# Graph attention over 16 images: setup bursts in pairs over two sets of PSUM banks, and loads and copies moved between queues

## The chip, the cores and the metric

The kernel runs on one core of a Trainium2 chip. A core has engines that run side by side, each in its own order: TensorE (PE, matmuls, with PEld for its weight loads), VectorE (DVE), ScalarE (ACT), GpSimd (POOL) and SyncE (SP), which here only issues DMA transfers. On-chip memory is SBUF; matmuls write to PSUM, which has eight banks of 512 floats in each of 128 partitions. The metric is the device time of one execution in microseconds (us).

## The reference

The input is 16 images of 512 rows and 512 features, one vector q of 512 for each image, and for each image an integer label array of 512 x 512 x 11. What is computed, cut to what matters:

```python
row_zero = v.sum(-1) == 0
q_exp = jnp.where(row_zero[..., None], 0.0, q[:, None, :])
self_feat = jnp.concatenate([v, q_exp], -1) @ W_self.T + b_self
output = self_feat
for d in range(2):                      # adj, and adj transposed
    A = (adj if d == 0 else jnp.swapaxes(adj, 1, 2))[:, :, :20, :]
    output += gat(self_feat, A.sum(-1), A @ w_bias + b_bias, Wq[d], ..., Wout[d], bout[d])
return v + relu(output)

def gat(x, cond, label_bias, ...):      # 16 heads of 32
    kv = x[:, :20]                      # the first 20 rows are the keys
    aff = einsum("bnhd,bmhd->bnhm", q, k) / sqrt(32)
    w = softmax(where(cond > 0, aff, NEG) + label_bias)
    return einsum("bnhf,hgf->bnhg", einsum("bnhm,bmf->bnhf", w, kv), Wout) + bout
```

So every image has 512 queries against 20 keys, 16 heads and two directions: 640 scores a row. The condition row_zero asks for each row of v whether its sum is zero; the kernel keeps that as "flags", one number for each row, by which q's part is multiplied.

## The kernel before

All arithmetic is float32 (F = 512 features are held as C = 4 chunks of 128 partitions). Nothing is scheduled by a planner: `manual_schedule` leaves each engine's instructions in the order in which they are written, and each DMA is issued by the engine whose queue it is written to. A helper `behind` gives a load on SP's queue another instruction to wait for, so that loads start in turn. An instruction that waits holds up all that follows on its engine or queue.

**The setup** (lines 458 to 777) loads the weights, computes the self features of the 16 x 20 key rows (`kv_terms`, L537), the 8 blocks of projected keys khD (`key_rows`, L588), and then, in 20 bursts, the keys multiplied back through Wq (`keys`, L676), so that the loop can take scores directly from self features. A burst is 25 or 26 units, a unit being 19 columns (keys 1 to 19 less key 0) of one image, direction, head group and feature chunk; its four heads are row-tiled matmuls with a contraction of 32 that run side by side in the array, 475 or 494 columns long. They write into two tiles of two PSUM banks each from the pool ps_s. ACT then scales and copies the pair of heads 0 and 1 (L691), DVE the pair of heads 2 and 3 (L693), into a stage tile st in SBUF. A stage is 32 units; when it is full, POOL copies image 0's part to g0 (L697) and SP stores image 1's part to g1_d (L698) and the other 14 images to g_d (L699), 1064 KB, in DRAM. There are 16 stages.

Between bursts PE does other work, here called filler, which is column-tiled (32 columns of output for each of four tiles) and writes to a pool of four more banks: the remaining key rows, `values` (L649: the keys' values through Wout, stored to vw_d), `bias_scores` (L624), and the block products of image 0 (L283). A string `plan` lists the filler behind each burst. Two of the fillers, `row_flags` of images 0 and 1 (L213), use the whole array: a 128 x 128 matrix of ones times the row sums (which POOL has added up in `row_sums`), so that each partition of a 512-column bank holds the sums of all rows; DVE's comparison with zero writes the flags nz[b], [128, 512], straight into SBUF (L215).

The values must reach bd_d in DRAM in block-diagonal form: `clear_first` writes zeros there (POOL's queue), and 12 DRAM-to-DRAM copies (`spill`, L187; the list `copies` from `blocks(0)`) put the values of the first five images in their places. Six of them are issued on POOL's queue in the setup (after bursts 14 to 19) and six in the loop.

**The loop** (lines 786 to 1006) goes over images b (16) and row tiles nt (4 of 128 rows). A row tile has 64 score matmuls into two banks (`scores`, L365, some 4 us) and a softmax: DVE adds the mask and bias (L379), takes the maximum (L383), subtracts it (L387), ACT exponentiates (L392), DVE sums and inverts (L415, L416), POOL multiplies (L417), DVE transposes (L424). In between PE makes the self features of image b + 1 by seven block products of Strassen's kind (`product`, L283, some 1.66 us each), which share four banks: products 1, 6, 7 and 4 add up in the pair ps_a, product 2 goes to ps_d, 5 and 3 to ps_c. After products 1, 6, 7 and 4 DVE reads the pair and adds flags times q (`partial`, L289) to give a block of the self features. The order is

```python
# nt == 2: scores(b, 2); product(b+1, 1); product(b+1, 2); weigh(b, 2) with partial(b+1, 0, 0) inside
# nt == 3: product(b+1, 6); normal(b, 2); partial(b+1, 0, 1); scores(b, 3); product(b+1, 7); product(b+1, 5); ...
```

and `attend` (L435, weights times values) of image b - 1 comes ahead of the scores of row tile 2. SP's queue carries, in the written order, the loads of labels (`load_adj`, L119), of bias scores (`load_cq`, L124), of x in two layouts (L107, L113), of keys g (`load_keys`, L135), values (L141) and flags (`load_nz`, L202), the zeros for the rest of bd_d (L157), copies (L187), and the stores of the result (L454). For images 2 and on the flags come from ACT's row sums: `row_mask` writes 512 of them to nz_d (L198) and `load_nz` reads them back to all partitions an image later.

## Time and profile before

| what | value |
|---|---|
| median of 3 runs | 583.28 us (582.72 to 583.82) |
| profiled execution | 582.57 us, span 580.7 us, granted clock 0.999 |
| busy share of PE, DVE, ACT, POOL | 99%, 84%, 68%, 70% |
| setup (to the first score matmul of the loop) | 91.3 us |
| bytes moved | 123.26 MB, 212 GB/s on average |

The span is that of the profiled instructions; the time of the execution includes what lies around it. A row of the timeline or of the chain begins with its start and its length in us, then the engine, the line and what is written from what. "SPq" and the like are an engine's queue of DMA issues: its length there is the time for which the issue occupied the queue, not the transfer's. In rows of groups, "busy, mean ns | idle before, releaser" tells the time and what the engine waited for; in those of one tile or line, three numbers are the least, median and greatest length in ns, followed by the starts of the first and the last. ps_k, ps_v, ps_nz, ps_a, ps_c, ps_d are the banks of key rows, values, flags and products; matmuls of float32 appear as two instructions each.

### The profile page before, as it was taken

The numbers are of one execution on the slowest core, as the hardware profiler recorded it, in microseconds if no ns is written. First come the engines' busy times: TensorE is split into PE (matmuls) and PEld (weight loads), VectorE is DVE, ScalarE is ACT, GpSimd is POOL, SyncE is SP. The second block draws the span as 40 slices with busy tenths as digits, with TensorE's granted clock in tenths as the row PEclk, the third lists the DMA queues.
The fourth block names the chain that finished last, engine by engine and source line by source line (L and its number), as shares of the span: only waits on it lengthen the run. The fifth ranks groups of instructions, "written<-read, shape, count | busy, mean of one in ns | idle before, by whom it ended". The sixth has DMA issues, their size and how long they took to land.

```text
span 580.7 us, 30994 instructions
## 1 busy us (share of the span) xinstructions
PE 574.0 (99%) x13496; PEld 431.6 (74%) x13496; DVE 489.8 (84%) x786; ACT 395.8 (68%) x1170; POOL 404.2 (70%) x383
## 2 busy tenths in 40 slices
PE   8999999999999999999999999999999999999996
PEld 6444458878878787878778787887887878787873
DVE  0475676979898989898999999898989898989896
ACT  1334454587877777778786868687887877777671
POOL 2626976748687776858585867786868677685875
PEclk9999999999999999999999999999999999999999
DMA  8998997857675767777576767566657666674404
GB/s 290 387 399 300 332 362 274 231 144 222 202 239 177 215 200 198 218 181 229 171 215 166 219 166 219 166 205 181 202 162 223 197 191 182 196 205 109 148 19 146
DMA packets 98787, 123.26 MB, mean 212 GB/s; under 512 B 18876, under 2 KB 66968, under 8 KB 96604
## 3 DMA queue, kind: packets, MB, share of 16 engines
q1 hardware_dynamic: 96124, 117.80, 65.5%
q0 software_dynamic: 1392, 2.43, 1.8%
q8 instruction: 106, 1.74, 1.2%
q10 hardware_dynamic: 1136, 1.06, 0.5%
q14 instruction: 29, 0.24, 0.1%
HBM read 82.30 MB, written 40.24 MB: 211 GB/s over the span
## 4 chain that ended last, share of the span: by engine, by line
PE 94%; DVE 3%; DMA 1%; issue 0%; POOL 0%; SPq 0%; ACT 0%; DVEq 0%; POOLq 0%; ACTq 0%
PE ps_s L365 45%; PE ps_a L283 19%; PE ps_c L283 9%; PE ps_o L435 5%; PE ps_d L283 5%; PE ps_v L649 3%; PE ps_k L588 3%; DMA ws_q<-in_wsT 1%; PE ps_kv L537 1%; DVE o L444 0%; PE ps_nz L213 0%; DVE o L1023 0%; DVE wt L424 0%; DVE ps_s L383 0%; DVE sm L415 0%
## 5 line engine op out<-in xcount | busy, mean ns | idle before, releaser
L365 PEld LDWEIGHTS ps_s<-g,sf 128*32 128x32 f32 x8192 | 263.0, 110 | 21.5 <-issue 13.9
L365 PE MATMUL ps_s<-g,sf 128*32 128x152 f32 x8192 | 278.1, 293 | 0.3 <-issue 0.2
L337 ACT COPY both<-add 32x80 f32<-32x80 f32 x512 | 130.9, 256 | 60.3 <-DVE add L328 54.4
L417 POOL TENSOR_TENSOR s<-s,sm 128x640 f32<-128x640 f32 x63 | 80.2, 1274 | 95.5 <-DVE sm L416 73.4
L344 POOL TENSOR_TENSOR full<-cq,both 128x640 f32<-128x640 f32 x64 | 100.3, 1567 | 27.1 <-issue 21.2
L317 ACT ACTIVATE prod<-adj,wb_sb 128x80 f32<-128x80 int32 x330 | 112.4, 432 | 0.0
L392 ACT ACTIVATE s<-s 128x640 f32<-128x640 f32 x63 | 46.5, 738 | 56.5 <-DVE s L387 56.1
L449 POOL TENSOR_TENSOR o<-o,x 128x512 f32<-128x512 f32 x60 | 76.6, 1299 | 0.0
L379 DVE TENSOR_TENSOR full<-ps_s,full 128x608 f32<-128x608 f32 x63 | 48.7, 773 | 22.5 <-PE ps_s L365 19.2
L283 PE MATMUL ps_a<-t,ws_s 128*32 128x246 f32 x1024 | 60.0, 371 | 0.0
L415 DVE TENSOR_REDUCE sm<-s 128x32 f32<-128x640 f32 x63 | 50.8, 807 | 10.6 <-ACT s L392 10.4
L383 DVE TENSOR_REDUCE ps_s<-full 128x32 f32<-128x640 f32 x63 | 52.2, 828 | 2.2
L424 DVE STREAM_TRANSPOSE wt<-s 128x640 f32<-128x640 f32 x63 | 52.8, 838 | 0.6 <-POOL s L417 0.6
L387 DVE TENSOR_TENSOR s<-full,ps_s 128x640 f32<-128x640 f32 x63 | 51.5, 818 | 1.1
L289 DVE SCALAR_TENSOR_TENSOR sf<-nz,qw,ps_a 128x246 f32<-128x246 f32 x128 | 51.6, 443 | 0.3
L283 PEld LDWEIGHTS ps_a<-t,ws_s 128*32 128x32 f32 x1024 | 33.9, 110 | 17.5 <-issue 0.9
L328 DVE TENSOR_REDUCE add<-prod 128x80 f32<-128x960 f32 x32 | 36.8, 1149 | 6.8 <-ACT prod L317 4.0
L446 ACT ACTIVATE o<-o,bo 128x512 f32<-128x512 f32 x60 | 38.2, 709 | 0.6 <-DVE o L444 0.6
L248 POOL TENSOR_TENSOR t<-x 128x492 f32<-128x492 f32 x32 | 36.7, 1148 | 1.6 <-DMA g_d<-st 1.5
L248 POOL TENSOR_TENSOR t<-x,t 128x492 f32<-128x492 f32 x32 | 36.7, 1148 | 1.3
L435 PE MATMUL ps_o<-wt,vd 32*32 32x512 f32 (+5 forms) x816 | 37.6, 578 | 0.0
L444 DVE TENSOR_TENSOR o<-ps_o,sf 128x512 f32<-128x512 f32 x60 | 36.7, 668 | 0.0
(225 smaller groups left out, 712.6 us busy)
## 6 DMA issues: line engine op xcount, KB each, us to landing
g<-g_d SPq DMA_DIRECT2D x60, 304.0 KB
g_d<-st SPq DMA_DIRECT2D x16, 1064.0 KB
out_T<-o SPq DMA_DIRECT2D x60, 256.0 KB
xn<-in_xn SPq DMA_DIRECT2D x56, 256.0 KB
x<-in_xT SPq DMA_DIRECT2D x56, 256.0 KB
adj<-in_adj SPq DMA_DIRECT2D x60, 220.0 KB
nz<-nz_d SPq DMA_DIRECT2D x14, 256.0 KB
wk<-in_wkT SPq DMA_DIRECT2D x2, 1024.0 KB
```

What stands on the lines that cost most here:

```text
L248: done["xsum"] = nc.gpsimd.tensor_sub(t, one, two)
L283: nc.tensor.matmul(to, lhs, x[:, k], start=start, stop=stop, skip_group_check=n != 2)
L289: done["partial"] = nc.vector.scalar_tensor_tensor(to[:, i], nzs[b][:, half(l)], qw[:, 2 * f + i, b : b + 1], parts[b, "a"][i][:, :HN], AL ...
L317: nc.scalar.activation(p[:, :, l], a[:, :, l], AF.Identity, scale=wb_sb[:, l : l + 1])
L337: done["spread"] = nc.scalar.copy(adds[b, h][bass.ts(a, R), :, g], add[r].rearrange("p (t m) -> p t m", t=2))
L344: done["full"] = nc.gpsimd.tensor_add(f, cqs[b].unsqueeze(1).to_broadcast(shape), adds[b, nt // 2][:, nt % 2].unsqueeze(2).to_broadcast(sh ...
L365: nc.tensor.matmul(to, sfs[b][:, k, bass.ds(nt * P + (2 * g + j) * R, R)], of, start=(onto is None and k == 0 and (whole or j == 0)), stop ...
L383: nc.vector.tensor_reduce(mx, f, AX.X, ALU.max)
L417: done["normal"] = nc.gpsimd.tensor_mul(s, s, sm.unsqueeze(3).to_broadcast(full))
L424: nc.vector.transpose(wts[b][:, nt], s.rearrange("p a h m -> p (a h m)"))
L435: nc.tensor.matmul(banks[a][bass.ds(at // 2 * DH, n * DH)].rearrange("p (t n) -> p t n", n=32), vd[r, bass.ds(at * DH, n * DH)], wt[r, :, ...
L449: nc.gpsimd.tensor_add(o[:, c], o[:, c], xs[b][:, c])
```

## The change

- The pool ps_s is opened after the setup. In the setup all eight banks form two pools of four single-bank tiles, `acc[0]` and `acc[1]`; a burst takes one set, a head to a bank.
- The bursts come as seven doubles and six singles: the string at the end of the diff lists them with their filler, "+" for a double. A double's second burst takes the other set, and the filler takes the set that was emptied first.
- Evictions go head by head in the order 0, 2, 1, 3 (ACT 0 and 1, DVE 2 and 3): 8 to 12 instructions a burst in place of 4 to 6.
- `row_flags` uses four column-tiled matmuls of 128 columns, compares a [128, 128] tile, writes 512 flags to nz_d, and `load_nz` reads them back. Image 0's are made in the setup; image 1's in the loop, at b = 0: written ahead of scores(0, 2), read back behind them.
- The loads of adj(0, 1) and x(1) and `clear_first` move to behind burst 14 (`later`). The 12 copies of `blocks(0)` are all issued on SP's queue, in row tile 0 of image 0, between the halves of load_adj(1, 0).
- `row_sums(1)` moves to the end of the setup; the pool xsum is opened ahead of work; `attend` does the runs of two first.

```diff
@@ -60,13 +60,13 @@
     load = ctx.enter_context(tc.tile_pool(name="load", bufs=2))
     sfp = ctx.enter_context(tc.tile_pool(name="sfp", bufs=3))
     msk = ctx.enter_context(tc.tile_pool(name="msk", bufs=2))
-    ps_s = ctx.enter_context(tc.tile_pool(name="ps_s", bufs=2, space=PSUM))
     acc = {}
 
     def bank(name, at=None):
 
-        tag = {} if at is None else {"bufs": 1}
-        return acc["pool"].tile([P, 512], F32, tag="acc" if at is None else f"acc{at}", name=name, **tag)
+        if at is None:
+            return acc[acc["from"]].tile([P, 512], F32, tag="acc", name=name)
+        return acc["pool"].tile([P, 512], F32, tag=f"acc{at}", name=name, bufs=1)
 
     ctx.enter_context(tc.manual_schedule())
 
@@ -208,11 +208,14 @@
         for k in range(2, C):
             nc.gpsimd.tensor_add(t, t, xs[b][:, k])
 
-    def row_flags(b):
-        ps = bank(f"ps_nz{b}")
-        nc.tensor.matmul(ps[:, :N], ones, rss[b], start=True, stop=True)
-        nzs[b] = load.tile([P, N], F32, tag="nz", name=f"nz{b}")
-        nc.vector.tensor_scalar(nzs[b], ps[:, :N], 0.0, None, ALU.not_equal)
+    def row_flags(b, at=None):
+
+        ps = bank(f"ps_nz{b}", at)
+        for a in range(HL):
+            nc.tensor.matmul(ps[bass.ts(a, R), :P], ones[:, :R], rss[b][:, bass.ts(a, P)], start=True, stop=True)
+        t = msk.tile([P, P], F32, tag="nzf", name=f"nzf{b}", bufs=1)
+        nc.vector.tensor_scalar(t, ps[:, :P], 0.0, None, ALU.not_equal)
+        nc.sync.dma_start(nz_d[b].rearrange("(a n) -> a n", a=HL), t[0:P:R])
 
 
     def weight_sums():
@@ -428,7 +431,7 @@
 
         wt = wts[b][:, tiles].rearrange("p t (g w) -> p (t g) w", g=HL)
         vd = vds[b].rearrange("p e i g -> p (e i g)")
-        for first, runs in ((True, ((0, 1, 0), (3, 1, 2), (4, 1, 2), (7, 1, 4))), (False, ((1, 2, 1), (5, 2, 3)))):
+        for first, runs in ((True, ((1, 2, 1), (5, 2, 3))), (False, ((0, 1, 0), (3, 1, 2), (4, 1, 2), (7, 1, 4)))):
             for at, n, j in runs:
                 for a in range(HL):
                     r = bass.ts(a, R)
@@ -455,7 +458,9 @@
         outs.clear()
 
 
-    with tc.tile_pool(name="setup", bufs=1) as sp, tc.tile_pool(name="ps_acc", bufs=4, space=PSUM) as acc["pool"]:
+    with tc.tile_pool(name="setup", bufs=1) as sp, tc.tile_pool(name="ps_0", bufs=4, space=PSUM) as acc[0], tc.tile_pool(
+        name="ps_1", bufs=4, space=PSUM
+    ) as acc[1]:
         wq_sb = sp.tile([P, 2, C, F], F32, name="wq_sb")
         wo_sb = sp.tile([P, 2, C, F], F32, name="wo_sb")
         khD = sp.tile([P, 2 * C, B * ND], F32, name="khD")
...
@@ -664,34 +668,36 @@
             stages = {"c": load.tile([P, 2, F], F32, tag="xn", name="c")}
             nc.gpsimd.memset(stages["c"][:, :, :BM], 0.0)
 
-            def keys(runs):
-
-
-                pairs = [ps_s.tile([P, 2, 512], F32, tag="s", name=f"ps_g{runs[0]}{i}") for i in range(2)]
+            def keys(runs, side):
+
+
+                acc["from"] = side
+                heads = [bank(f"ps_g{runs[0]}{hl}") for hl in range(HL)]
                 at = 0
                 for fc, hg, d, lo, hi in runs:
                     n = (hi - lo) * ND
                     for hl in range(HL):
                         r = bass.ts(hl, DH)
                         nc.tensor.matmul(
-                            pairs[hl // 2][:, hl % 2, at : at + n], wq_sb[r, d, hg, bass.ts(fc, P)],
+                            heads[hl][:, at : at + n], wq_sb[r, d, hg, bass.ts(fc, P)],
                             khD[r, d * C + hg, lo * ND : hi * ND], start=True, stop=True,
                         )
                     at += n
-                at = 0
-                for fc, hg, d, lo, hi in runs:
-                    n = (hi - lo) * ND
-                    if (fc, hg) not in stages:
-                        stages[fc, hg] = sg.tile([P, B, HL, 2, ND], F32, tag="st", name=f"st{fc}{hg}")
-                    st = stages[fc, hg]
-                    for half in range(2):
-                        to = st[:, lo:hi, bass.ts(half, 2), d].rearrange("p b h m -> p h b m")
-                        of = pairs[half][:, :, at : at + n].rearrange("p h (b m) -> p h b m", m=ND)
-                        if half == 0:
+                for hl in (0, 2, 1, 3):
+                    at = 0
+                    for fc, hg, d, lo, hi in runs:
+                        n = (hi - lo) * ND
+                        if (fc, hg) not in stages:
+                            stages[fc, hg] = sg.tile([P, B, HL, 2, ND], F32, tag="st", name=f"st{fc}{hg}")
+                        to = stages[fc, hg][:, lo:hi, hl, d]
+                        of = heads[hl][:, at : at + n].rearrange("p (b m) -> p b m", m=ND)
+                        if hl < 2:
                             nc.scalar.activation(to, of, AF.Copy, scale=SCALE)
                         else:
                             nc.vector.tensor_scalar(to, of, SCALE, None, ALU.mult)
-                    at += n
+                        at += n
+                for fc, hg, d, lo, hi in runs:
+                    st = stages[fc, hg]
                     if d == 1 and hi == B:
                         to, of = g0[:, fc, bass.ts(hg, WD // C)], st[:, 0].rearrange("p h d m -> p (h d m)")
                         nc.gpsimd.tensor_copy(to, of)
...
@@ -731,56 +726,59 @@
                         runs.append((fc, hg, d, b, b + 1))
                 del units[: 25 + (len(bursts) % 5 < 3)]
                 bursts.append(runs)
-            rest = [(d, hg) for hg in range(C) for d in range(2)]
-            first = None
-            for n, runs in enumerate(bursts):
-                for i in range(len(rest)):
-                    if i < (4 if n == 0 else 1) or any(fc == 0 and (d, hg) == rest[0] for fc, hg, d, _, _ in runs):
-                        key_rows(*rest.pop(0))
-                if n == 4:
-                    values(*steps["v"].pop(0)[1])
-                keys(runs)
-                if rest:
-                    for kind in "mm" if n else ():
-                        f, args = steps[kind].pop(0)
-                        f(*args)
-                    continue
-                first = n if first is None else first
-                for kind in plan[n - first] if n - first < len(plan) else ():
+            copies = []
+
+            def later():
+
+                load_adj(0, 1)
+                load_x(1)
+                clear_first()
+                copies.extend(blocks(0))
+
+            steps = {
+                "r": [(key_rows, (d, hg)) for hg in range(C) for d in range(2)],
+                "b": [(biases, ())],
+                "c": [(bias_scores, (d,)) for d in range(2)],
+                "m": [(bias_terms, (d, c)) for c in range(C) for d in range(2)],
+                "n": [(row_flags, (0,))],
+                "p": [(block_product, (n,)) for n in (1, 2, 6, 7, 5, 4, 3)],
+                "v": [(values, (t, (d,), k)) for t in range(2) for d in range(2) for k in range(C)],
+                "w": [(values, (2, (0, 1), k)) for k in range(C)],
+                "R": [(row_sums, (1,))],
+                "M": [(mask_mul, (0, h)) for h in range(2)],
+                "C": [(mask_count, (0, h)) for h in range(2)],
+                "S": [(mask_sum, (0, 0))],
+                "T": [(mask_spread, (0, 0, (i,))) for i in range(4)],
+                "L": [(load_cq, (0,))],
+                "N": [(load_nz, (0,))],
+                "D": [(later, ())],
+                "F": [(new_self, (0,))],
+                "X": [(x_sum, (0, i)) for i in range(1, 5)],
+                "A": [(full_add, (0, 0))],
+            }
+
+            def do(kinds):
+
+                for kind in kinds:
                     f, args = steps[kind].pop(0)
                     f(*args)
-                if n == 7:
-                    mask_mul(0, 0)
-                if n == 8:
-                    mask_count(0, 0)
-                if n == 10:
-                    mask_sum(0, 0)
-                    load_cq(0)
-                if n == 7:
-                    clear_first()
-                if n == 9:
-                    row_sums(1)
-                    copies = blocks(0)
-                if n > 13:
-                    spill(1, nc.gpsimd)
-                if n == 11:
-                    new_self(0)
-                    for i in range(1, 5):
-                        x_sum(0, i)
-                if 10 < n < 15:
-                    mask_spread(0, 0, (n - 11,))
-                if n == 14:
-                    mask_mul(0, 1)
-                if n == 15:
-                    mask_count(0, 1)
-                if n == 17:
-                    full_add(0, 0)
-
+
+            do("rrrr")
+            side = 0
+            for kinds in "+mrmmrmmr +mrnmmvvvvb +ccvvvvM +vvvvCN +vvvvSL +wwwwFXXXXT +pT pTD pT p pAM pC pR".split():
+                keys(bursts.pop(0), side)
+                if kinds[0] == "+":
+                    keys(bursts.pop(0), 1 - side)
+                    side = 1 - side
+                acc["from"] = 1 - side
+                do(kinds.strip("+"))
+
+    ps_s = ctx.enter_context(tc.tile_pool(name="ps_s", bufs=2, space=PSUM))
     acc["pool"] = ctx.enter_context(tc.tile_pool(name="ps_loop", bufs=1, space=PSUM))
     soft = ctx.enter_context(tc.tile_pool(name="soft", bufs=2))
     gp = ctx.enter_context(tc.tile_pool(name="gp", bufs=2))
+    xsum = ctx.enter_context(tc.tile_pool(name="xsum", bufs=1))
     work = ctx.enter_context(tc.tile_pool(name="work", bufs=2))
-    xsum = ctx.enter_context(tc.tile_pool(name="xsum", bufs=1))
     ident = ctx.enter_context(tc.tile_pool(name="one", bufs=1)).tile([P, P], F32, name="ident")
 
     with tc.manual_schedule():
@@ -859,7 +857,7 @@
                         turn(*prev)
                     full_add(b, 1)
                     if b == 0:
-                        spill(6, nc.gpsimd)
+                        spill(12)
                     if more:
                         x_sum(b + 1, 1)
                         load_adj(b + 1, 0, done["xsum"], slice(1, 2))
@@ -930,8 +928,12 @@
                         load_xn(b + 2, 1, done["sum"], slice(1, 2))
                     if more:
                         load_keys(b + 1, range(1), done["normal"])
+                    if b == 0:
+                        row_flags(1, 3)
                     for g in range(2):
                         scores(b, nt, g, ps[g])
+                    if b == 0:
+                        load_nz(1)
                     if more:
                         product(b + 1, 1)
                         product(b + 1, 2)
```

More of the change, by code (lines that the diff above doesn't have):

```diff
@@ L482, in gat_kernel @@
             nc.vector.memset(ones, 1.0)
-            ps_q = ps_s.tile([P, 2, 512], F32, tag="s", name="ps_q4")
-            nc.vector.memset(ps_q[:, 0], 0.0)
+            acc["from"] = 0
+            ps_q = [bank(f"ps_q{i}") for i in range(2)]
+            nc.vector.memset(ps_q[0], 0.0)
             nc.vector.memset(bqbd, 0.0)
```

32 lines of the change are left out of this document (10 added, 22 removed).

## The prediction

> **What bounds the kernel now.** I read the page first: the busy shares and the chain that ended last.
>
> ```profile
> PE 574.0 (99%) x13496; PEld 431.6 (74%) x13496; DVE 489.8 (84%) x786; ACT 395.8 (68%) x1170; POOL 404.2 (70%) x383
> ```
>
> ```profile
> PE 94%; DVE 3%; DMA 1%; issue 0%; POOL 0%; SPq 0%; ACT 0%; DVEq 0%; POOLq 0%; ACTq 0%
> ```
>
> TensorE (PE) is busy for 574.0 of 580.7 us, and the chain runs through it for 94%. So a microsecond counts only if PE loses or gains it. Two questions are left: how much PE time the new setup saves, and whether PE now waits for something that was always early. For both I read the chain in order of time, from the setup into the loop.
>
> ```profile
> 54.66 1.85 PE ps_v L649 x16
> 56.51 1.06 PE ps_nz L213 x2
> ...
> 69.07 1.00 PE ps_v L649 x8
> 70.07 1.06 PE ps_nz L213 x2
> ...
> 91.33 3.85 PE ps_s L365 x114
> ...
> 104.66 1.66 PE ps_a L283 x31
> 106.32 1.66 PE ps_d L283 x32
> 107.98 1.62 PE ps_a L283 x30
> ```
>
> The loop begins with scores(0,0) at 91.33, which I call S0. Products 1, 2 and 6 of image 1 run without a gap from 104.66 on, so product 6 starts at S0+16.65. The stretches of ten microseconds (columns: sum and busy time of PE, PEld, DVE, ACT, POOL with their instructions, granted clock, DMA share, GB/s) say the same of the setup: PE is full while DVE and ACT have room, and the DMA engines are saturated without holding PE up.
>
> ```profile
> 80.00:90.00 10.00, 10.00 (x188) 6.09 (x184) 7.68 (x16) 3.75 (x10) 6.13 (x10) 1.00 1.00 369
> ```
>
> **Double bursts.** The timeline of PE shows burst 0 (heads 0 and 1): the starts of its two passes of 304 columns, of the first of its two of 190, and what comes behind.
>
> ```profile
> 26.03 0.53 PE L676 MATMUL s_g(0, 0, 0, 0, 16)0_324<-khD,wq_sb 32*128 32x304 f32 x2
> ...
> 26.39 0.42 PE L676 MATMUL s_g(0, 0, 0, 0, 16)0_324<-khD,wq_sb 32*128 32x304 f32 x2
> ...
> 26.64 0.33 PE L676 MATMUL s_g(0, 0, 0, 0, 16)0_324<-khD,wq_sb 32*128 32x190 f32 x2
> ...
> 27.07 2.36 PE L588 MATMUL ps_k<-kvT,wk 128*32 128x320 f32 x32
> ```
>
> From start to start the first pass takes 0.36 and the second 0.25, so entering the row-tiled form costs 0.11. The two of 190 columns, 0.16 each at the rate of the second pass, take 0.43 together, so leaving it costs 0.11 too. The filler pays as well: eight of its instructions take 1.00 us and 16 take 1.85, so eight more cost 0.85 and each filler has 0.15 on top. Two bursts in a row save 0.22 + 0.15 = 0.37; seven doubles save 2.6 us.
>
> **Flags.** Each full-array ps_nz matmul takes 1.06 (rows above), 2.12 for both. In its place come four column-tiled ones of 128 columns: eight instructions of 512 columns cost 0.85, a quarter of that is 0.2. The setup gains 2.12 - 0.2 = 1.9 us; image 1's 0.2 now lies in the loop.
>
> **What the double bursts add.** The evictions go head by head, so there are twice as many.
>
> ```profile
> L691 ACT ACTIVATE st<-_g(0, 0, 1, 10, 16)0_359 x3: 308/368/690, 30.6 to 31.4; 128x228 f32<-128x228 f32 x1, 128x608 f32<-128x608 f32 x1, 128x152 f32<-128x152 f32 x1
> L693 DVE TENSOR_SCALAR st<-_g(0, 0, 1, 10, 16)1_360 x3: 306/396/782, 30.7 to 31.7; 128x228 f32<-128x228 f32 x1, 128x608 f32<-128x608 f32 x1, 128x152 f32<-128x152 f32 x1
> ```
>
> By the slope between 228 and 608 columns, a head's 304 and 190 columns cost some 0.70 on ACT and 0.80 on DVE once their overlap is taken off. A double leaves ACT four heads (2.8 us) and DVE four (3.2). Doubles with three or four groups of filler last 5 us and cover that; three places remain. (1) The first filler takes head 0's bank of the first set: that burst ends 0.93 after the double's start, ACT begins 0.25 later (my allowance for the signal) and is done at about 1.95, and PE wants the bank at 1.86. With waits for its signal that is 0.1 to 0.2 seven times: 0.7 to 1.4, I take 1.0. (2) Burst 14 follows the last double after one product (1.66 in the loop) and takes the set that DVE empties last: 0.93 + 0.25 + 4 x 0.80 = 4.4 against 1.86 + 0.1 + 1.66 = 3.6, so 0.8. (3) The loop's score banks are now the setup's banks, and scores(0,0) waits for the last join of image 0:
>
> ```profile
> L299 DVE TENSOR_TENSOR sf<-ps_c,sf 128x492 f32<-128x492 f32 x1 | 0.7, 670 | 0.6 <-PE ps_c L283 0.6
> ```
>
> Its 0.67 plus signals is 0.8. With 0.15 for burst 1, which meets its key rows sooner, the costs are 2.75, and the setup gains 2.6 + 1.9 - 2.75 = 1.8 us. If (1) and (2) hide it is 3.6, and with the rest hidden too 4.5 at most; if each double's filler waits as long as it saved (0.37), 0.2. The loads, zeros and copies that leave the setup free queues and DMA, which PE did not wait for: nothing. The order of attend's two halves changes no count of switches: nothing.
>
> **What the move puts into SP's queue.** Here is the term that decides. Twelve value copies stood in POOL's queue; now all stand in SP's, in row tile 0 of image 0. SP also carries the new path of image 1's flags: row_flags(1) writes nz_d, load_nz(1) reads it back, and both come after row tile 1's loads. partial(1,0,0) on DVE multiplies by those flags, and product 6 needs the banks which that partial empties; product 6 stands right behind product 2, ahead of scores(0,3). Queued behind on DVE are the softmax of row tile 2 and all that follows. Formerly the flags lay in SBUF from the setup on. What SP did from row tile 0 on, and the copies' own rows:
>
> ```profile
> 95.32 5.42 SPq L119 DMA_DIRECT2D adj<-in_adj  x2
> 100.83 0.38 SPq L157 DMA_DIRECT2D bd_d<-zero  x1
> 101.30 1.94 SPq L124 DMA_DIRECT2D cq<-cq_d  x4
> ...
> 106.19 1.55 SPq L113 DMA_DIRECT2D xn<-in_xn  x3
> ```
>
> ```profile
> L187 SPq DMA_DIRECT2D bd_d<-vw_d x12: 775/802/1084, 187.4 to 257.9; - x12
> ```
>
> ```profile
> 217.71 0.80 SPq L187 DMA_DIRECT2D bd_d<-vw_d  x1
> 218.62 0.45 SPq L119 DMA_DIRECT2D adj<-in_adj  x1
> ```
>
> A copy holds SP for 0.91 from its issue to the next. Against S0: the first half of adj at 4.0, done at 4.45; twelve copies, 10.9, to 15.4; the second half 0.45, a zero 0.47, four cq 2.0, two adj 0.9, a zero 0.47, three xn 1.65, to 21.3; one g load 0.47, to 21.8. That is where the write of nz_d is issued. Three rows price the rest: write and read-back in the steady loop (the instructions on that tile, with their first and last start), a load of 256 KB at the start of the kernel, and the partial.
>
> ```profile
> L198 SPq DMA_DIRECT2D nz_d<-nz x1: 590/590/590, 305.5 to 305.5; - x1
> L202 SPq DMA_DIRECT2D nz<-nz_d x1: 327/327/327, 309.7 to 309.7; - x1
> ```
>
> ```profile
> 0.72 0.91 ACTq L499 DMA_DIRECT2D ws_v<-in_wsT  x2
> ```
>
> ```profile
> 4.26 0.50 PEld L537 LDWEIGHTS ps_kv<-xkv,ws_v 128*128 128x128 f32 x2 [0.15 <-DMA ws_v<-in_wsT]
> ```
>
> ```profile
> 106.71 0.84 DVE L289 SCALAR_TENSOR_TENSOR sf<-nz,qw,ps_a 128x246 f32<-128x246 f32 x2
> ```
>
> ```profile
> 106.12 1.27 POOL L417 TENSOR_TENSOR s<-s,sm 128x640 f32<-128x640 f32 x1
> ```
>
> Write to read-back 4.2, the load 3.5, the partial 0.84: 21.8 + 8.6 = S0+30.4. PE is through product 2 at 16.65 + 0.2 = 16.9. It stands still for 13.5 us. No later stage gives this back, because PE sets the pace of all of them. Ends: the POOL row above is the multiplication that the g load waits for; it ends at 107.39, S0+16.1, so even with copies at no cost the write comes at 16.5, and with the shorter signals of a quiet queue (3.1 for the write, an estimate at three quarters of 4.2) the partial is done at 16.5 + 3.1 + 3.5 + 0.84 = 24.0: 7.1 us. At the slowest (1.08 a copy, 2 more) it is 15.5.
>
> By the Trainium skill, "DMA: Bandwidth & Descriptors", section "Issuing engines are not separate DMA queues", starting transfers on another engine changes only the time that the sequencer needs to initiate them, which it calls usually small beside the transfer; by that rule the copies would add little and the sum would be near the lower end, some 6 us less, at the quick copies' time below. The trace does not bear out the "usually small": 0.80 us for each copy, twelve times over, is more than the whole way from a write to its read-back.
>
> **After the stall.** PE's first matmuls in the kernel are slow:
>
> ```profile
> 1.05 3.35 PE L496 MATMUL ps_warm<-ones 128*128 128x128 f32 x14 [1.05 <-DVE ones L482]
> ```
>
> ```profile
> 11.24 2.39 PE ps_kv L537 x8
> ```
>
> 14 instructions of 128 columns in 3.35 us are 1.87 ns a column; 8 of 320 in 2.39 are 0.93. A start from rest loses half of 3.35, 1.7 us. After 13 us at rest I take the same 1.7; 0 is the other end. The Trainium skill, "TensorE: Matmul & The Clock Gate", section "What's actually happening", has the array fall to half clock after an idle window of about 3.4 us; no long rest inside this run shows it.
>
> **Sum.** -1.8 (setup) + 0.2 (flags in the loop) + 13.5 (stall) + 1.7 (slow restart) = +13.6. The profiled execution took 582.57, 0.7 below the median of 583.28 and 1.9 above its span of 580.7; against it that is 596.2, and against the median 596.9 us.
>
> **Rivals.** *Copies leave SP quickly* (0.4 each, as its other transfers): 12 x 0.5 less of stall leaves 7.5, and the time is 590.9. For it: other transfers take 0.33 to 0.45. Against it: twelve SP rows of this very copy, none under 0.775. Chance 0.14. *No restart loss*, all else as forecast: 595.2, inside the range; 0.15. *Setup gains nothing*, so that the change does not do what it says: each double's fillers wait for ACT as long as the switch had cost, 1.6 more, 598.5; for it: ACT gets the critical bank only 0.1 late by my sum, so a few tenths decide; 0.12. *Faster*: the flags of image 1 are on chip when product 6 comes, that is, SP gets to the write of nz_d by S0+9 (8.6 us before the end of product 2). Then only setup terms remain: 583.3 - 1.8 + 0.2 = 581.7, 579.0 at best. It decides at a stall of 1.6. For it: nothing but the chance that I misread which transfers stand ahead of that write. Against it: the g load ahead of it waits for POOL until S0+16.1 by the row above, whatever the copies cost. Chance 0.06.
>
> **How the numbers follow.** The forecast proper gets 0.51, its variants 0.27, the quick copies 0.14, faster 0.06, and 0.02 for a cancelling middle. Measurement can tell about 0.2%, 1.2 us. The range leaves out the faster case: the shortest stall, no restart loss and the fullest setup gain give 583.3 - 4.5 + 0.2 + 7.1 = 586.1; the longest stall with restart loss and a setup gain of 0.2 gives 600.5.
>
> **What would show it.** Right: the loop starts near 89.5; PE has one idle gap of 11 to 15 us, between product 2 and product 6 of image 1, ended by DVE's L292 partial, itself ended by the load of nz; twelve copies in SP's rows at 0.8 each; ps_nz only 0.2; from there on the chain as before, shifted. Wrong: product 6 follows product 2 without a gap; or the gap is there but ends long before S0+24; or the setup ends later than 91.

## The result and the profile after

The changed kernel takes 604.38 us (median of 5 runs, 603.20 to 605.69) against 582.96 for the kernel before: 1.0366 times as long, with a 95% interval from 1.0348 to 1.0385. I had forecast 596.9 with a range from 586.1 to 600.5. The direction and the loop's stall are as forecast; the setup is not, and the time lies outside the range. First the page after, in the order in which the page before was read: busy shares, the granted clock in 40 slices, the chain.

```profile
PE 576.8 (96%) x13508; PEld 436.0 (72%) x13508; DVE 491.8 (82%) x834; ACT 397.8 (66%) x1218; POOL 395.2 (66%) x371
...
PEclk9999799959999999999999999999999999999999
...
PE 86%; DMA 3%; DVE 3%; issue 3%; POOL 3%; ACT 1%; SPq 0%; DVEq 0%; POOLq 0%; ACTq 0%
```

PE is busy for 576.8 us, only 2.8 more than before, in a span that is 21.9 longer (602.6). So the time went into waits, and the two slices with a lower clock (7 and 5 tenths, about 60 and 120 us) say where to look. The chain in order of time, from the loop's start:

```profile
97.94 7.68 PE ps_s L368 x227
105.62 1.59 issue
107.21 1.09 PE ps_s L368 x26
...
108.71 0.83 DVE s L390
...
111.68 1.27 POOL s L420
...
116.74 1.28 POOL s L420
118.02 1.51 POOL full L347
119.53 8.67 issue
128.20 3.51 PE ps_a L286 x32
131.70 5.08 PE ps_s L368 x128
136.79 1.66 PE ps_a L286 x32
```

The loop starts at 97.94, where it was 91.33 before and 89.5 in my forecast. Product 6 of image 1 starts at 128.20, which is 30.3 after the loop's start; the forecast said 30.4. It and scores(0,3) take 3.51 and 5.08 in place of 1.66 and 4.13. In order of place: 6.6 are lost in the setup (97.94 - 91.33); 13.6 up to product 6 (30.3 in place of 16.65 after the loop's start: 11.0 of idle PE right ahead of it, 1.6 and 0.9 in two gaps before, 0.2 for the flags' matmuls, less the 0.24 of a gap before); 2.8 in the slow restart. That is 23.0, and 21.9 of it are left at the end; where the other 1.1 comes back was not traced.

On DVE and SP the stall shows as I had read it out of the queue:

```profile
108.71 0.82 DVE L390 TENSOR_TENSOR s<-full,ps_s 128x640 f32<-128x640 f32 x1 [4.71 <-PE ps_nz L215]
...
127.62 0.85 DVE L292 SCALAR_TENSOR_TENSOR sf<-nz,qw,ps_a 128x246 f32<-128x246 f32 x2 [10.01 <-DMA nz<-nz_d]
```

```profile
101.56 12.24 SPq L187 DMA_DIRECT2D bd_d<-vw_d  x12
...
119.63 0.38 SPq L135 DMA_DIRECT2D g<-g_d  x1
120.11 0.57 SPq L218 DMA_DIRECT2D nz_d<-nzf  x1
124.55 0.33 SPq L202 DMA_DIRECT2D nz<-nz_d  x1
```

The twelve copies hold SP for 12.24 us, the flags are written at 120.11, their read-back is issued 4.4 later, and DVE waits 10.0 for it. But the first DVE row is a wait that I had not seen: the softmax of row tile 0 waits 4.7 us for the flags' matmul, which comes after scores(0,1).

The setup, in stretches of ten microseconds (sum, busy time of PE, PEld, DVE, ACT, POOL, then granted clock, DMA share, GB/s), before and after:

```profile
30.00:40.00 10.00, 9.98 (x156) 4.98 (x152) 8.70 (x22) 3.86 (x10) 2.85 (x5) 1.00 1.04 406
40.00:50.00 10.00, 10.00 (x121) 3.79 (x113) 6.60 (x16) 4.37 (x12) 3.44 (x6) 1.00 0.84 319
50.00:60.00 10.00, 10.00 (x118) 4.18 (x118) 5.53 (x10) 4.88 (x10) 8.75 (x14) 1.00 0.97 315
```

```profile
30.00:40.00 10.00, 10.00 (x160) 5.63 (x156) 9.20 (x26) 3.46 (x14) 2.96 (x5) 1.00 0.75 295
40.00:50.00 10.00, 9.45 (x112) 3.64 (x104) 4.98 (x16) 4.63 (x15) 4.77 (x9) 1.00 0.72 271
50.00:60.00 10.00, 10.00 (x140) 4.74 (x140) 7.78 (x23) 4.73 (x20) 9.53 (x15) 1.00 0.79 214
60.00:70.00 10.00, 6.22 (x60) 3.35 (x56) 4.45 (x12) 3.08 (x14) 1.63 (x4) 0.76 0.99 360
70.00:80.00 10.00, 10.00 (x140) 5.29 (x136) 5.46 (x17) 5.15 (x21) 5.06 (x6) 0.90 0.76 264
...
90.00:100.00 10.00, 7.95 (x156) 5.23 (x155) 6.33 (x16) 4.25 (x15) 6.02 (x7) 1.00 1.01 390
```

PE is nearly as full as before until 60 (one wait of 0.55 from 40 to 50). What is new is the DMA column: from 30 to 60 the engines moved 10.4 MB before (406, 319 and 315 GB/s for 10 us each) and 7.8 MB after. The missing 2.6 MB come later, when the engines are full for most of the time (0.99 to 1.01 in three of the four stretches from 60 to 100); at 390 GB/s they take 6.7 us. That this is nearly the 6.6 by which the setup is late proves nothing by itself: from 70 to 80 the engines had room again (0.76, and 264 GB/s where the kernel before moved 348). The chain of the setup shows where PE meets late transfers:

```profile
39.49 3.43 PE ps_v L653 x32
...
55.22 10.14 DMA vw_d<-v
...
65.48 0.70 DVE v L659
...
68.37 5.42 PE ps_v L653 x32
...
81.97 9.94 DMA adj<-in_adj
```

A store of values takes 10.14 us to land, DVE's next copy waits for its buffer, PE stands for 3.8 us behind it and comes back slow: 32 instructions of `values` take 5.42, where 32 such instructions had taken 3.43. Later the labels that were moved behind burst 14 take 9.94 us, ACT waits for them, and its evictions with it.

### The profile page after: what moved, and what is told of

Same layout as the page of the kernel before. It is cut to its first block, busy times and chain, and to the rows that moved or that the text cites. A ratio compares the mean times of both kernels' runs of the same rounds, so it can differ in the third digit from the quotient of the medians.

```text
span 602.6 us, 31141 instructions
## 1 busy us (share of the span) xinstructions
PE 576.8 (96%) x13508; PEld 436.0 (72%) x13508; DVE 491.8 (82%) x834; ACT 397.8 (66%) x1218; POOL 395.2 (66%) x371
## 3 DMA queue, kind: packets, MB, share of 16 engines
q10 hardware_dynamic: 1136, 1.06, 0.5%
## 4 chain that ended last, share of the span: by engine, by line
PE 86%; DMA 3%; DVE 3%; issue 3%; POOL 3%; ACT 1%; SPq 0%; DVEq 0%; POOLq 0%; ACTq 0%
PE ps_s L368 42%; PE ps_a L286 17%; PE ps_c L286 9%; PE ps_o L438 5%; PE ps_d L286 4%; PE ps_k L592 3%; PE ps_kv L542 2%; DMA vw_d<-v 2%; DMA adj<-in_adj 2%; PE ps_v L653 1%; POOL cq_d L639 1%; POOL s L420 1%; PE ps_warm L503 1%; POOL full L347 1%; ACT st L695 0%
## 5 line engine op out<-in xcount | busy, mean ns | idle before, releaser
L382 DVE TENSOR_TENSOR full<-ps_s,full 128x608 f32<-128x608 f32 x63 | 48.6, 772 | 24.5 <-PE ps_s L368 24.5
```

## The experiments

Two questions: why the setup is late, and what makes the stall. Each kernel is the changed one with the edit shown, unless said otherwise. A time is a median; two or three numbers behind it in brackets are the ratio to the kernel before and its 95% interval. The median of the kernel before lay between 582.93 and 583.57 beside these runs. Where only a profile is quoted, note that the loop starts between 97.0 and 100.0 in the seven profiles (the changed kernel's and six of the kernels below) that share its setup, so a difference below 1.5 us in one profile is not read.

**A third buffer for the values** (e1).

```diff
-v = msk.tile([P, H * S], F32, tag="full", ...)           # and the other two tiles of this tag
+v = msk.tile([P, H * S], F32, tag="full", ..., bufs=3)
```

> The changed kernel (604.4 us), with a third buffer for the tiles that hold the values on their way to DRAM (tag full, 3 in place of 2). Theory: in the setup DVE's copy of values (1,1) waits for the buffer until the store of values (0,1) has landed at 65.4, PE stands 3.8 us behind it and then runs at a low granted clock for some 2.7 us; without the wait the time falls by 5 to 7, to about 598. Rival: the setup is held by the DMA engines, which two stores in a row fill; then the wait comes back at the next buffer or at the stages, and the time falls by less than 1.5.

603.54 us (1.0335, 1.0317 to 1.0352): the rival. PE's 3.8 us wait is gone, and the loop starts at 97.2 all the same. Who waits now, between 58 and 98 us:

```profile
ACT prod L316 <- DMA adj<-in_adj: 4.6, 1, 4.6
...
ACT st L695 <- DMA g_d<-st: 4.1, 4, 1.7
DVE st L697 <- DMA g_d<-st: 4.1, 3, 1.5
```

The evictions wait for stages whose stores have not landed. Whichever buffer is freed, the next late transfer is behind it.

**Copies, ones, and both.** The matrix of ones lies in memory that the loop's first softmax tile and image 1's sums take over, so these wait for its last reader. That reader was in the setup; the change made it `row_flags(1)`, in row tile 2.

```diff
 # e2: the copies
-full_add(b, 1); if b == 0: spill(12)                      # row tile 0
+if b == 0: load_nz(1); spill(12)                          # row tile 2, behind the read-back
 # e3: the ones
-ones = sp.tile([P, P], F32, name="ones")
+ones = const.tile([P, P], F32, name="ones")
 # e4: both
```

> The changed kernel, with the 12 value copies issued on SP behind the read-back of image 1's flags. My prediction's theory: the copies set the time of the flags' write; without them ahead of it the write goes out about 10 us sooner, bounded by POOL, and the time falls by 5 or more, to 599 or less. Rival, from the trace after: the g load ahead of the write waits for POOL's multiplication of row tile 1, which ends at 118.0 because row tile 0's softmax on DVE waited 4.7 us for the flags' matmul; the write can come only 1.6 us sooner and the time falls by 1 to 2, to about 603.

> The changed kernel, with the matrix of ones kept in a place of its own for the whole run, so that the softmax tile of row tile 0 and the x sums of image 1 no longer lie on it and need not wait for the flags' matmul. Theory: DVE's wait of 4.7 and POOL's of 6.3 go, but the copies still hold SP's queue until 113.8, so the write of the flags stays where it is and the time changes by less than 1, 604. Rival: if that wait alone set the write, the time falls by 4 to 5, to about 600.

> Both edits of the two kernels before. Theory: each of the two holds the write of the flags at nearly the same time, so only both together move it, to 16.5 to 17.5 us after the loop's start in place of 22.2; the stall shortens by about 5 and the time falls to about 599. Rival: a third wait (the labels of image 1 on ACT, the zeros) stands at nearly the same time too, and less than 2 is gained.

602.52, 605.41 and 599.23 us. Of the edits alone, the copies bring 1.9 and the ones nothing (1.0 more, with intervals that overlap); both bring 5.2, as expected. In the kernel with both, the write of the flags goes out 16.45 us after that loop's start (98.93), behind the g load that waits for POOL, the bound that the prediction had worked out for copies at no cost (16.5). The read-back follows 4.07 later, not the 3.1 that the prediction had taken for a quiet queue, and product 6 starts 24.5 after the loop (forecast for this case 24.0):

```profile
114.90 0.38 SPq L136 DMA_DIRECT2D g<-g_d  x1
115.38 0.53 SPq L219 DMA_DIRECT2D nz_d<-nzf  x1
119.45 0.33 SPq L203 DMA_DIRECT2D nz<-nz_d  x1
```

So the copies were a sufficient cause of the late write and not the only one: POOL's multiplication was nearly as late, through the ones. In the changed kernel it ended 20.1 after the loop's start (118.02), and SP reached the g load at 21.7.

**Matmuls in the stall** (e5).

```diff
 product(b + 1, 1); product(b + 1, 2); new_self(b + 1)
+if b == 0:
+    idle = bank("ps_idle", 3)
+    for _ in range(10):
+        nc.tensor.matmul(idle, ws_v[:, 0, :P], xs[1][:, 0], start=True, stop=True)
```

> The changed kernel, with ten more matmuls of 128 x 512 over the full array (results unused, some 10.6 us) between product 2 and product 6 of image 1, where PE stands still. Theory: PE comes out of the stall at full rate, product 6 takes 1.66 in place of 3.51 and scores(0,3) 4.13 in place of 5.08, so the time falls by 2.5 to 3, to about 601.7, for more work. Rival: the slow rows come from something else (operands, weights late): no change, or a rise as far as the added work outlasts the stall.

603.96 us: the time did not fall as expected. The rows did:

```profile
117.53 8.78 PE ps_idle L944 x20
126.31 3.18 issue
129.50 1.87 PE ps_a L286 x32
131.37 4.13 PE ps_s L368 x128
```

Kept at work, PE does scores(0,3) in 4.13 in place of 5.08 and product 6 in 1.87 in place of 3.51: 2.6 us of the slow restart come from the rest. In this profile the loop started 0.7 later, the flags came 0.6 later and attend had a gap of 0.8, which takes most of it back; that these three follow from the edit is not shown.

**The flags first** (e6). `row_flags(1)` behind scores(0,0), read back ahead of row tile 1, the copies behind scores(0,2), the ones kept.

> The changed kernel, with image 1's flags made behind scores(0,0), written and read back ahead of the copies, the copies behind scores(0,2), and the ones kept. Theory: the flags are on chip before product 2 ends, the stall and its slow restart go, the loop loses nothing against the kernel before and the time falls by 15 to 16, to about 589. Rival: the waits move to the next late transfer (keys or labels of image 1) and more than 3 of it stays.

597.64 us: 6.7 less, where 15 to 16 were expected. The stall is gone but for 0.6 us ahead of product 6, and the rival's case came too. The copies now stand ahead of the last g loads of image 1, and scores(1,0) waits 5.3 us for those and restarts slowly (6.47 for 120 instructions).

**attend in the old order** (e7).

> The changed kernel, with the two halves of attend in the order of the kernel before. Theory: the order costs nothing, 604.4 within 0.5. Rival: the new order brings the gain of 0.4 us between the first row tiles and the end (22.3 behind after image 1, 21.9 at the end); then the time rises by 0.3 to 1.

604.29 us against 604.38: the order costs nothing.

**All found waits out, and the loads back.** e8 adds the third buffer and the early labels to the flags first. e10 is the changed kernel with x(1), the labels and the first zeros (2.1 MB) in their old places. e11 joins both, with the copies behind the last g load.

```diff
 # e10
 def later():
-    load_adj(0, 1); load_x(1); clear_first()
     copies.extend(blocks(0))
+load_x(1); load_adj(0, 1)                                 # behind the weights
-+ccvvvvM
++ccvvvvMZ                                                 # Z: clear_first
```

> The kernel with the flags first, and also a third buffer for values and the labels of image 0's second half loaded early, as before. Theory: all the waits found are out, what is left is the setup's own gain of 1 to 2 us: 581 to 582, faster than the kernel before by 0.2 to 0.4%. Rival: with the labels back among the first loads, the DMA engines make the stores and the values late again and the setup stays 2 to 5 us longer: 585 to 588.

> The changed kernel, with x(1) and the labels adj(0,1) loaded behind the weights and the first zeros written behind burst 7, as in the kernel before (2.1 MB that the change moved behind burst 14, where the DMA engines are full). Theory: the setup is late because DMA had 25% idle from 30 to 60 us and a backlog of ten microseconds a transfer from 80 to 100; with the 2.1 MB back in the early stretch the loop starts 4 to 6 us sooner, at 92 to 94, and the time falls by 4 to 6, to about 599. Rival: the setup is late because of the wait for the values' buffer (3.8 us at 62) and its slow restart; that is ahead of burst 14 and stays, and the time falls by less than 2.

> The kernel with all waits out (flags first, ones kept, third buffer for values), with the loads and zeros in their old places and the 12 copies behind the last g load of image 1. Theory: no backlog is left at the loop's start, the gaps in which PE waits for its own instructions and the g load's wait of 2.9 go, and the setup keeps its gain of 1 to 2: 581 to 582.5. Rival: the doubles hand over stages two at a time, the DMA engines idle early and the stores end late whatever is loaded when: the loop starts at 92 or later and the time is 584 to 587.

591.45, 600.60 and 589.65 us. The loads alone bring 3.8, and the loop starts 3.4 sooner, at 94.56: a little less than expected, the values' wait being left (3.5). e8 missed its theory and its rival: its loop starts at 92.97, and then PE has 3.6 us of gaps that end on no event and waits 2.9 us for a g load. With everything found repaired (e11) the kernel is still 1.06% slower than the one before (1.0080 to 1.0132): the loop starts at 95.36, after PE has waited 3.0 us for evictions whose stages were late, at another place than in e1. I had expected 581 to 582.5, with 584 to 587 for the rival. (The expectation speaks of gaps in which PE waits for its own instructions: that is a reading of gaps that end on no event, and no run tests it.)

**Singles in place of doubles** (e12), on the same two sets of banks.

```diff
-+mrmmrmmr +mrnmmvvvvb +ccvvvvMZ +vvvvCN +vvvvSL +wwwwFXXXXT +pT pTD pT p pAM pC pR
+mr mmrmmr mr mnmvvvvb ccvv vvMZ vv vvCN vv vvSL ww w wFXXXXT pT pTD pT p pAM pC pR
```

> The kernel of the run before, in 20 single bursts with the same filler divided over them, on the same two sets of four banks. Theory: each double saves 0.37 us of switches, so singles are 2 to 3 us slower than the run before. Rival: with singles the stages come evenly, the stores start sooner and the switches are paid back: within 0.7 of the run before, or faster.

589.50 us: the same as the doubles. The loop starts at 92.22, 3.1 sooner than with doubles; attend of image 0 then waits 3.5 us for values, whose copies came last on SP, which blurs the comparison of times. The next kernels put the copies back on POOL's queue.

**Half the bytes.** What was left was the DMA engines themselves. Of these four kernels two store all of each stage (g4 in singles, g4d in doubles) and two only half of it (h4, h4d), so that the scores of images 9 to 15 use other images' keys; the copies are on POOL.

```diff
-nc.sync.dma_start(g_d[C * fc + hg], st[:, 2:])
+nc.sync.dma_start(g_d[C * fc + hg, :, :7], st[:, 2:9])
-src = g1_d if b == 1 else g_d[:, :, b - 2]
+src = g1_d if b == 1 else g_d[:, :, (b - 2) % 7]
```

> The kernel in single bursts with all waits out, with the 12 copies back on POOL's queue, six in the setup and six in the loop as in the kernel before. Theory: attend of image 0 waited 3.5 us for values whose copies came last on SP, and restarted slowly; both go, the loop is as in the kernel before and the time is 584 to 585. Rival: POOL's 8 us of issuing delays its softmax work at the loop's start, and the time stays above 587.

> The fourth of the set: doubles with all stores, copies on POOL, all found waits out. Theory: with the DMA engines full the doubles lose again what they save: the loop starts at 92 to 95, no sooner than the singles' 92.7, and the time is 586 to 589. Rival: with the copies off SP the doubles keep 2 us, 584 or less.

> The kernel of the run before, but of each stage only the keys of images 2 to 8 are stored, and read again for images 9 to 15 (the later images' scores are computed with other images' keys): 16 stores of 0.53 MB in place of 1.06, 8.5 MB less, 22 us of the DMA engines at 390 GB/s. Theory (DMA is the setup's second limit): the loop starts 1 to 2 us sooner than with all bytes, by 90.5 or sooner. Rival (PE and its evictions alone set the setup): within 0.5 of the run before.

> The same half stores (and the same wrong keys for the later images) with the seven double bursts of the change. Theory: with room on the DMA engines the doubles' PE saving shows: no stall in the setup, the loop starts 2 to 2.6 us sooner than with singles and half stores, near 88. Rival: the doubles' evictions (DVE 3.2, ACT 2.8 us a double) hold PE whatever the stores do, and the loop starts within 0.7 of the singles or later.

| | all bytes stored | half stored |
|---|---|---|
| singles | 586.29, loop at 92.67 (g4) | 585.09, loop at 91.56 (h4) |
| doubles | 587.41, loop at 93.93 (g4d) | 581.82, loop at 89.09 (h4d) |

With half the bytes the doubles are 3.3 us faster than the singles, and the loop starts 2.47 us sooner, 2.6 by the prediction's term. With all the bytes they are 1.1 slower by the medians, which the noise does not tell from equal (1.0058 to 1.0104 against 1.0039 to 1.0072). PE's instructions are the same in both columns. (g4 at 586.29 missed its 584 to 585: POOL is late with the sums for image 1's flags, and PE waits 1.0 us for them. h4's loop was expected by 90.5.)

Where the doubles lose their gain shows in g4d's chain:

```profile
58.89 12.43 DMA g_d<-st
71.42 0.40 ACT st L697
71.87 3.51 PE ps_a L287 x32
```

A store of a stage takes 12.43 us to land, ACT waits for the stage tile, and PE, which rests 3.18 us behind ACT, does product 1 of image 0 in 3.51 in place of 1.87. These 3.2 + 1.6 are the 4.8 by which its loop starts later than h4d's. The stage tiles are four; whether more of them would do as well as fewer bytes was not tried.

**The changed kernel with half the bytes, and no other edit** (a2).

> The changed kernel with one edit: of each stage only the keys of images 2 to 8 are stored, and read again for images 9 to 15 (later images' scores use other images' keys), 8.5 MB less through the DMA engines in the setup. Theory: with room on the DMA engines the setup's stalls go without any other repair (values' buffer, labels, stages), and the loop starts at 89 to 90.5, where my prediction had it, in place of 97.9; the loop's stall stays, so the time falls by 7 to 8.5, to 596 to 597.5. Rival: the order of POOL's queue alone makes the values' buffer late; the stall of 3.8 at 62 and its slow restart stay, and less than 4 is gained.

594.09 us, 10.3 less, more than expected: 9.0 by the loop's start, 0.3 up to product 6 and 0.9 in the restart behind it. The setup's stalls go at once, the values' wait at 62 among them, without any of the repairs; what is left of PE's waits there are 0.6 at the first evictions and the 0.8 of the join. The loop's stall stays. PE's timeline, with the idle time ahead of an instruction in brackets:

```profile
88.92 8.47 PE L368 MATMUL ps_s<-g,sf 128*32 128x152 f32 x256 [0.77 <-DVE sf L302]
98.56 4.34 PE L368 MATMUL ps_s<-g,sf 128*32 128x152 f32 x128 [0.94 <-DVE s L390]
118.88 3.51 PE L286 MATMUL ps_a<-t,ws_s 128*32 128x246 f32 x32 [12.66 <-issue]
```

The loop starts at 88.92 (forecast 89.5), product 6 starts 30.0 after it (forecast 30.4), and the first 256 score instructions run through without the gap of 1.59. The order of POOL's queue is the same, so it is not what made the values' store late: the slowest of the eight takes 5.6 us from issue to landing here, 10.8 in the changed kernel and 6.8 in the kernel before.

Beside this kernel the 9.0 us of the changed one can be placed: 3.8 are the rest at 62, 3.2 the slow matmuls behind it (product 1 of image 0 starts at 75.77 in place of 68.76), 1.2 a wait for ACT at 93 and 0.8 the burst behind that.

**The flags alone** (g2), in the kernel before: column-tiled, written and read back in the setup, both images.

> The kernel before with one part of the change: the flags of images 0 and 1 by column-tiled matmuls, written to DRAM and read back in the setup (two more loads of 256 KB on SP, behind bursts 10 and 14). By my prediction's PE row it saves 2.12 - 0.4 = 1.7 us: 581.5. Theory that the DMA engines bound the setup too: two loads of 256 KB cost some 1.3 us of them and SP waits for the write's landing, so half of it or all is lost: 582.5 to 583.5.

585.22 us (1.0032, 1.0021 to 1.0044): slower, where PE's row promised 1.7 and the other theory 582.5 to 583.5. The loop starts at 91.04, only 0.3 sooner (0.7 us goes to a wait for ACT, whose stage was held by a store that took 10.92 us to land), and then PE has 2.9 us of gaps in the first scores that end on nothing the profile shows:

```profile
PE ps_s L368 <- issue: 2.9, 2, 1.7
```

In the kernel before that gap was 0.24. At the first of the two the DMA share is 1.04, at the second it falls from 0.80 to 0.11. What causes them is not shown.

## Why the prediction was wrong where it was

**The step that failed** stands in its first part and in the sum of the double bursts: the DMA engines "saturated without holding PE up", and the moved loads, zeros and copies at "nothing". The row was right (DMA share 1.00), the reading was not: PE did not wait then, but the engines had no room to catch up. Full engines that nobody waited for were a second limit, close behind the first. The change let them idle for a quarter of the time from 30 to 60 us and asked for the missing 2.6 MB later. The setup's term was -1.8 and came out at +6.6; the sign that the prediction had named, a setup that ends later than 91, was there. With half the bytes and no other edit it is 88.92 - 91.33 = -2.4, near the forecast, so PE's side of that sum was about right in total and the missing term was DMA: 9.0 us by the loop's start. It was not right term by term: 2.75 were put down for waits and costs, and a2 shows waits of 0.56 and 0.77. Of the 9.0, the moved loads and zeros account for 3.4 (e10; 3.8 of the time). The rest is not divided. Stores that come in lumps are a candidate: at all bytes the loop of the singles starts 3.1 sooner in one pair (e12 and e11), but only 1.3 in the other (g4 and g4d). And the lull from 50 to 60 us, where 212 GB/s were moved in e10 and 315 in the kernel before, is there in singles too (208 in e12), so it has a further cause that was not looked for.

**Double bursts.** 0.37 a double, 2.6 for seven: measured 2.47 from one profile each, with room on the DMA engines only. The wait of scores(0,0) for the last join was forecast at 0.8 and is 0.77 to 0.79. The wait of 0.8 ahead of burst 14 did not show in the changed kernel.

**Flags.** The matmuls do shrink, from 1.06 to 0.22 each; alone they brought no time. In that kernel the two 256 KB loads and the write went through engines whose share was 0.86 to 1.02 from 60 to 95 us; that this is why is not shown.

**The copies and the stall.** The queue on SP held: write at 21.8 forecast, 22.2 measured; read-back after 4.2, measured 4.4; partial done at 30.4, product 6 at 30.3. That accuracy was partly luck. The copies took 1.02 each and not 0.91, and POOL, which I had bounded by the kernel before (16.1), ended at 20.1, nearly as late as the copies, through a dependency that neither the diff nor the rows of before show: a tile of ones that shares memory with the loop's tiles and had got a later reader. The stall is 11.0 and not 13.5, because 2.5 us of gaps came ahead of it.

**The restart.** Forecast 1.7, measured 1.85 + 0.95 = 2.8; 2.6 of it went when PE was kept busy. The granted clock was 0.50 from 120 to 130 and 0.82 from 130 to 140. The size is not fixed: behind rests of 10.4 to 13.1 us in the kernels that share this stall, product 6 and scores(0,3) lost 1.6 (e2), 1.9 (a2) and up to 2.9 (e10), so a forecast of 1.7 lay inside what occurs. The Trainium skill, "TensorE: Matmul & The Clock Gate", section "What's actually happening", puts the fall to half clock at an idle window of about 3.4 us. Here a rest of 3.8 us in the setup was followed by a clock of 0.50 from 66 to 72 us (5.42 for 3.43), and rests of 3.0 in e11 and 3.2 in g4d were followed by 0.50 too, so here the measured rests go below that figure. What I had not counted is that the setup could have such a rest too.

**The Trainium skill's rule on issuing engines** ("DMA: Bandwidth & Descriptors", section "Issuing engines are not separate DMA queues") I had weighed for the copies alone. Its first half, that all transfers run on the same 16 engines whoever issues them, is the one that bears on the setup. The runs agree: halving the stores, which SP issues, brought the slowest of the values' stores, which POOL issues, from 10.8 us to 5.6. Moving x(1), the labels and the zeros to another time was worth 3.8 us.

**The rivals.** *Copies leave SP quickly* is refuted (12.24 for twelve). *Setup gains nothing* came true, and more, but not by its mechanism: ACT's critical bank was not it, as the doubles with half stores show: PE waits for an eviction there once, for 0.55 us. *Faster* did not happen. The range ended at 600.5 because it had no term in which the setup loses: its worst setup still gained 0.2.

No version here beats the kernel before with all its work done; the nearest is the flags alone (g2), 0.3% slower.

## What to carry to other kernels

Where PE is 99% busy and the DMA engines are 100% busy beside it, both are limits: cost every edit on both, in bytes by time as well as in instructions. Before moving a transfer later, add up what the engines have to move after that point; before making one engine's work come in larger lumps, ask which queue runs empty between the lumps. And when an instruction gets a later place, look for what shares memory with its operands: here a softmax waited 4.7 us for that.

## What the runs showed of the hardware

Behind PE's rest of 3.8 us in the setup the granted clock was 0.50 from 66 to 72 us, and behind the 11 us in the loop it was 0.50 up to 132; matmuls whose results nobody reads, put into the rest, kept it at 1.00. Rests of 3.0 us (e11, 0.50 from 74 to 78) and 3.2 us (g4d, 0.50 from 72 to 74) were followed by the low clock too, but the 3.2 us that were left in e5 were not. In e3, e4, e6 and e7 waits of 1.3 to 1.4 us at 91 to 94 were followed, 1 to 2.5 us after PE had gone on, by 0.50 for three to six us; the 1.2 us at that place in the changed kernel were not.

In the loop's first scores PE had gaps of 1.1 to 1.9 us that end on no event of the profile (the changed kernel, e2, e5, e8, g2). In the changed kernel the gap began at a DMA share of 1.02 and the share fell to 0.27 and 0.08 within it. But the first gap of g2 began and ended at 1.04, and e3 and g4 ran their first scores at shares of 0.95 to 1.10 with no such gap, so full engines alone do not make it. With half stores the first 256 score instructions had none. That PE waits there for its own instructions, which also come by DMA (the page's row "q8 instruction"), was not tested.
